# Token rows of a recurrence: identity products with the gate's columns beside them, or transpositions and products of eight columns

## The chip, the cores and the metric

The kernel runs on one core of a Trainium2 chip. The metric is device time in microseconds (us), the median of the runs of one kernel; lower is better.

## What is computed

A recurrence makes 2048 token states of width 256, a gate picks two of eight experts for each, and the experts' outputs are added to x. Cut to what matters:

```python
def step(prev_h, xw_t):                      # xw_t = (x @ Wx + b) at step t
    next_h = jnp.tanh(xw_t + prev_h @ Wh)
    return (next_h, next_h)
_, hs = jax.lax.scan(step, h0, jnp.swapaxes(xW, 0, 1))
...
logits = x_flat @ gate_w.T                   # x_flat: the states hs, [2048, 256]; gate_w: [8, 256]
top_v, top_i = jax.lax.top_k(logits, 2)
probs = softmax(top_v)
...
hidden = silu(x_flat @ wge.T) * (x_flat @ wue.T)
out   += we[:, None] * (hidden @ wde.T)      # we: this expert's weight for each token
...
return x + out
```

## The kernel before, in words

**The recurrence.** The long sequence is cut in 64 chunks for each of the two batches, so one step advances 128 states at once. The states lie transposed: two tiles of 128 features by 128 states (`hall[k][:, r, :]`, k = 0, 1). A step (loop at L668) is four products of 128 columns with `Wh` in two accumulators (L675), and two tanh on ACT (L694), which write the next states. Steps 8 to 27 use float16, the rest float32. From step 48 on the states of each step are kept: step 48 + r yields token tile r, r = 0 to 15.

**From states to rows.** One step after a tile's states exist, `route_tile` (L379) makes token rows of them. Its two products (L385) take the states as the stationary operand and `ig[:, k, :]` as the moving one, 136 columns: an identity of 128 columns, which turns the states, and the gate's eight columns beside it. The order in `ig` is identity and gate for k = 0, gate and identity for k = 1, so that both products write the same eight columns of one PSUM tile, 128 to 135, and the logits are summed there; columns 0 to 127 and 136 to 263 hold the two halves of the token's row. ACT then copies all 264 columns to SBUF (L387), to `gr["rows"]`. For tile 14, `before_copy` puts two transpositions of rows that were gathered earlier (`early_turn`, L516, L219), their cast on ACT and a subtraction on DVE ahead of that copy.

**What follows.** The tiles are routed in four groups (5, 3, 5 and 3 tiles). For each group DVE finds the two best logits (`route_max`, `route_choice`), ACT and DVE make the weights, PE counts the tokens of each expert with small float16 products (`route_position`, L433) and finds their places with others (`route_slots`, L479); SP's queue writes the rows to a table in DRAM (`rows_out`, L417), and POOL gathers from it by index (L493). The gathered rows are transposed again for the experts (`transpose_tokens`, L219), where each product is split in three terms (L759 for gate and up, L995 for down), and POOL adds the results to the output (L500).

**Order.** Each engine runs its instructions in the program's order. That order is written out by hand: `at(step, f)` files a function under a step number, and `run(step)` issues what is due, in the order of the numbers. `route_tile` for tile r stands at r + 49, so it is issued after the products, tanh and seeds of step r + 49; tile 15 is issued after the loop, ahead of the experts' first products. PSUM tiles for `route_tile` are `ptr`, two in turn. The lines touched by the change, and those next to it on PE, are L675 (recurrence), L385 (rows and logits), L433 and L479 (places), L219 (transpositions), L759 (the experts' first products). ACT, DVE and POOL instructions mostly appear as L57, that of a helper.

Of the kernel before, what the change touches and what calls it, by code (L numbers as in the profile page):

```python
# [19 lines left out]
P = 128  # L20
# [4 lines left out]
E = 8  # L25
# [35 lines left out]
def rnn_moe(ctx, tc, xP, cP, xT, xrows, h0T, Wx, Wh, b, gw, W, out):  # L61
    nc = tc.nc
    pe = tc.keep_in_program_order
# [12 lines left out]
    ig = cst.tile([P, 2, P + E], F32, name="ig")  # L76
    ident = cst.tile([P, P], F32, name="ident")
# [76 lines left out]
    def ptr_tile():  # L154
        return pl.ptp.tile([P, 512], F32, name="ptr", tag="ptr")
# [15 lines left out]
    def flat(t):  # L171
        return t.rearrange("p a c -> p (a c)")
# [29 lines left out]
    hall = [flat(t).bitcast(F32).rearrange("p (r c) -> p r c", r=R) for t in early["gu_g"]]  # L202
# [176 lines left out]
    def route_tile(gr, r, before_copy=lambda: None):  # L379
        i = r - gr["r0"]  # L380
        if i == 0:
            gr["mx"] = rt.tile([P, gr["n"], 8], F32, name="mx")
        pt = ptr_tile()[:, 0:ROW]
        for k in range(2):
            pe(nc.tensor.matmul(pt[:, k * P : (k + 1) * P + E], lhsT=hall[k][:, r, :], rhs=ig[:, k, :], start=(k == 0), stop=(k == 1), skip_group_check=True))  # L385
        before_copy()
        act.copy(gr["rows"][:, i, :], pt)  # L387

# [218 lines left out]
    for g, gr in enumerate(groups):  # L607
        for r in range(gr["r0"], gr["r0"] + gr["n"]):
            at(r + 49, route_tile, gr, r, *((lambda: early_turn(1),) if r == 14 else ()))
            at(maxima[r], route_max, gr, r)  # L610
# [57 lines left out]
    for s in range(S0, 64):  # L668
# [31 lines left out]
        if s in range(40, 48, 2):  # L700

            pt = ptr_tile()[:, 0:64]
# [585 lines left out]
```

## Time and profile before

| | us |
|---|---|
| median of 3 runs | 378.67 (378.03 to 378.75) |
| the profiled execution | 374.34 |
| its span in the profile | 372.5 |
| PE busy | 360.6 (97%) |
| PE weight loads busy | 344.6 (92%) |
| DVE busy | 221.4 (59%) |
| ACT busy | 198.6 (53%) |
| POOL busy | 121.4 (33%) |
| PE's share of the chain that ended last | 95% |

The profiled execution is one execution, 4.3 us shorter than the median of the runs; sums made from its rows stand against its own time. PE means TensorE's passes, PEld its weight loads, which overlap the passes. A pass's record lasts much longer than the distance to the next pass, since passes are pipelined. DVE is the vector engine, ACT the scalar engine, POOL the general one, SP the engine that issues plain DMAs. L385 is line 385 of the kernel. The chain that ended last is followed back from the end: at each step to what released it.

### The profile page before, as it was taken

Reading aid. Unit: us, or ns where it says so; the run is one execution under the profiler, and the core shown is the slowest. Engines: PE = TensorE matmul, PEld = TensorE weight load, DVE = VectorE, ACT = ScalarE, POOL = GpSimd, SP = SyncE. Lnnn points to the kernel's source line nnn. Section 1 sums busy time; section 2 is a strip of 40 time slices with the busy share of each in tenths; the row PEclk is TensorE's granted clock in tenths of the full one; section 3 lists DMA queues with packets and bytes.
Section 4 is the critical chain, followed back from the end, with each engine's and each line's share of the span. In section 5 each row is a group of like instructions: output and inputs, shape, how many; then the busy total and the mean of one; then the engine's idle time right before and its main releaser. Section 6 shows DMA issues by size and latency. Waiting matters only on the chain.

```text
span 372.5 us, 7262 instructions
## 1 busy us (share of the span) xinstructions
PE 360.6 (97%) x2743; PEld 344.6 (92%) x2743; DVE 221.4 (59%) x541; ACT 198.6 (53%) x458; POOL 121.4 (33%) x133
## 2 busy tenths in 40 slices
PE   7999999999999999999999999999999999999990
PEld 6999999999898889999999999999999999999890
DVE  6858737786577666745547554666646645663420
ACT  5776667634557446645456545556464465463320
POOL 3694001211872322862252503331033051005042
PEclk9999999999999999999999999999999999999997
DMA  8943234231482716745155333445215243004022
GB/s 263 472 173 123 111 108 117 69 80 31 80 282 61 246 45 191 147 173 141 31 141 143 60 113 101 81 143 143 94 25 138 95 147 39 2 0 53 0 24 35
DMA packets 17805, 42.11 MB, mean 113 GB/s; under 512 B 3995, under 2 KB 12243, under 8 KB 14643
## 3 DMA queue, kind: packets, MB, share of 16 engines
q1 hardware_dynamic: 11314, 32.59, 25.3%
q0 software_dynamic: 6448, 8.99, 14.2%
q8 instruction: 23, 0.38, 0.4%
q14 instruction: 20, 0.16, 0.1%
HBM read 35.15 MB, written 9.04 MB: 119 GB/s over the span
## 4 chain that ended last, share of the span: by engine, by line
PE 95%; DMA 1%; ACT 1%; POOL 1%; SPq 0%; issue 0%; POOLq 0%; ACTq 0%
PE pgu_t L759 49%; PE yb L995 21%; PE pgu_t L675 11%; PE ptr L328 3%; PE ptr L385 2%; PE ptr L219 2%; PE yb L946 2%; PE pgu_t L995 2%; DMA gu_u<-in_xP_dram 1%; PE ptr L995 1%; POOL out_dram L500 1%; PE pgu_t L310 1%; PE yb L479 0%; ACT gu_g L57 0%; PE yb L433 0%
## 5 line engine op out<-in xcount | busy, mean ns | idle before, releaser
L995 PE MATMUL yb<-wd,hh 128*128 128x256 f32 (+3 forms) x496 | 84.5, 283 | 0.5 <-ACT hh L57 0.5
L57 DVE TENSOR_TENSOR g<-g,pgu_t 128x256 f32<-128x256 f32 (+7 forms) x96 | 49.2, 512 | 59.1 <-PE pgu_t L759 51.4
L500 POOL DMA_INDIRECT out_dram<-y,si x27 | 44.4, 1646 | 108.3 <-ACT y L57 103.7
L57 ACT CAST hh<-g 128x256 fp32r<-128x256 f32 (+7 forms) x92 | 43.9, 477 | 64.4 <-DVE g L57 59.5
L759 PE MATMUL pgu_t<-xhi,gu_g 128*128 128x256 f32 (+7 forms) x384 | 76.9, 322 | 0.0
L759 PE MATMUL pgu_t<-xhi,gu_u 128*128 128x256 f32 (+7 forms) x384 | 76.7, 321 | 0.0
L57 ACT ACTIVATE g<-pgu_t 128x256 f32<-128x256 f32 (+7 forms) x96 | 44.0, 459 | 60.0 <-PE pgu_t L759 59.2
L995 PEld LDWEIGHTS yb<-wd,hh 128*128 128x128 f32 (+3 forms) x496 | 72.5, 185 | 2.1 <-ACT hh L57 0.7
L759 PEld LDWEIGHTS pgu_t<-xhi,gu_u 128*128 128x128 f32 x384 | 61.0, 188 | 3.7
L759 PEld LDWEIGHTS pgu_t<-xhi,gu_g 128*128 128x128 f32 x384 | 58.5, 189 | 2.3 <-ACT xhi L57 0.2
L57 DVE TENSOR_TENSOR hl<-g,hh 128x464 fp32r<-128x464 f32 (+5 forms) x52 | 30.5, 587 | 31.5 <-ACT hh L57 30.1
L493 POOL DMA_INDIRECT xg<-rows_d,gi x27 | 30.8, 1142 | 56.1 <-DVE cm L872 23.2
L759 PE MATMUL pgu_t<-xlo,gu_g 128*128 128x256 f32 (+7 forms) x192 | 46.2, 321 | 0.0
L759 PE MATMUL pgu_t<-xlo,gu_u 128*128 128x256 f32 (+7 forms) x192 | 46.1, 321 | 0.0
L995 PE MATMUL yb<-wd,hl 128*128 128x256 f32 (+3 forms) x152 | 42.7, 281 | 0.0
L759 PEld LDWEIGHTS pgu_t<-xlo,gu_g 128*128 128x128 f32 x192 | 32.4, 188 | 1.9
L759 PEld LDWEIGHTS pgu_t<-xlo,gu_u 128*128 128x128 f32 x192 | 32.3, 188 | 2.0
L675 PE MATMUL pgu_t<-h,wh 128*128 128x128 f32 (+1 forms) x224 | 28.8, 264 | 0.6 <-DVE wh L57 0.6
L995 PEld LDWEIGHTS yb<-wd,hl 128*128 128x128 f32 (+3 forms) x152 | 27.8, 183 | 0.0
L57 DVE TENSOR_TENSOR hh<-g,hh 128x256 fp32r<-128x256 f32 (+1 forms) x40 | 16.9, 424 | 17.8 <-ACT hh L57 16.8
L57 DVE TENSOR_TENSOR gu_u<-raw,gu_u 128x1024 fp32r<-128x1024 f32 (+1 forms) x18 | 20.3, 1127 | 0.9 <-ACT gu_u L57 0.9
L57 DVE TENSOR_TENSOR wd<-raw,wd 128x1024 fp32r<-128x1024 f32 (+1 forms) x18 | 19.9, 1105 | 0.9 <-ACT wd L57 0.9
(179 smaller groups left out, 478.8 us busy)
## 6 DMA issues: line engine op xcount, KB each, us to landing
raw<-in_W_dram SPq DMA_DIRECT2D x24, 1024.0 KB, 4.9
gu_u<-in_xP_dram SPq DMA_DIRECT2D x8, 256.0 KB, 4.8
rows_d<-gu_u SPq DMA_DIRECT2D x4, 320.0 KB
rows_d<-gu_u SPq DMA_DIRECT2D x4, 192.0 KB, 3.0
out_dram<-in_xrows_dram SPq DMA_DIRECT2D x1, 512.0 KB, 16.9
xg<-rows_d,gi POOLq DMA_INDIRECT x27
out_dram<-y,si POOLq DMA_INDIRECT x27
small<-in_cP_dram SPq DMA_DIRECT2D x1, 267.0 KB
```

Of the source, the lines that this page charges most:

```text
L57: return lambda *a, **k: self.tc.keep_in_program_order(f(*a, **k))
L219: pe(nc.tensor.transpose(pt[:, m, j, :], tiles[i][:, k * (P + E) : k * (P + E) + P], ident))
L310: pe(nc.tensor.matmul(bq(acc[s % 2][j])[:, :, sh:64], lhsT=wx16[:, k, j * P : (j + 1) * P], rhs=bq(x16[n][:, k, s % 2 * P : (s % 2 + 1) * ...
L328: pe(nc.tensor.matmul(pt, lhsT=wxs[a][:, k, j * P : (j + 1) * P], rhs=xparts[q % 2][c][:, k, :], start=(i == 0), stop=(i == len(terms) - 1)))
L385: pe(nc.tensor.matmul(pt[:, k * P : (k + 1) * P + E], lhsT=hall[k][:, r, :], rhs=ig[:, k, :], start=(k == 0), stop=(k == 1), skip_group_ch ...
L493: nc.gpsimd.indirect_dma_start(out=xg, out_offset=None, in_=rows[:, :], in_offset=bass.IndirectOffsetOnAxis(ap=idx, axis=0),)
L500: return nc.gpsimd.indirect_dma_start(out=out[:, :], out_offset=bass.IndirectOffsetOnAxis(ap=idx, axis=0), in_=y, in_offset=None, compute_ ...
L675: pe(nc.tensor.matmul(acc[s % 2][j], lhsT=w[:, k, j * P : (j + 1) * P], rhs=prev[k], start=False, stop=True, skip_group_check=True))
L759: pe(nc.tensor.matmul(pt, lhsT=a[i], rhs=b[j], start=(first and i + j + n == 0), stop=(j == 1 and n == len(lhs_rhs) - 1), skip_group_check ...
L946: pe(nc.tensor.matmul(yt, lhsT=wd[b][:, s, d * P : (d + 1) * P], rhs=u.hid[s][a], start=(s == 0 and n == 0), stop=(s == NIC - 1 and n == 2 ...
L995: pe(nc.tensor.matmul(yt[0:w, :], lhsT=h[a][:, i * P : i * P + w], rhs=wd[b][:, ic, :], start=(ic == 0 and first and n == 0), stop=(ic == ...
```

## The change

The two products of 136 columns become two products of eight columns (the gate's logits) and two transpositions of 128 columns (the row's halves), in the same PSUM tile and the same columns of it. The stationary operand of all four is the same pair of state tiles; the moving operand is a slice of `ig` that holds only the gate's columns, or `ident`, an identity tile that exists already. The copy on ACT and all that follows are as before; in the changed kernel, lines after this function are two higher (L385 becomes L385 for the products and L387 for the transpositions; L675 becomes L677, L759 becomes L761).

```diff
         pt = ptr_tile()[:, 0:ROW]
         for k in range(2):
-            pe(nc.tensor.matmul(pt[:, k * P : (k + 1) * P + E], lhsT=hall[k][:, r, :], rhs=ig[:, k, :], start=(k == 0), stop=(k == 1), skip_group_check=True))
+            pe(nc.tensor.matmul(pt[:, P : P + E], lhsT=hall[k][:, r, :], rhs=ig[:, k, (1 - k) * P : (1 - k) * P + E], start=(k == 0), stop=(k == 1), skip_group_check=True))
+        for k in range(2):
+            pe(nc.tensor.transpose(pt[:, k * (P + E) : k * (P + E) + P], hall[k][:, r, :], ident))
         before_copy()
         act.copy(gr["rows"][:, i, :], pt)
```

## The prediction

> **What bounds the kernel now.** I read the page first (PE busy 97% of the span, the chain that ended last 95% PE), then the stretch in which the changed function runs. It is called once per token tile, sixteen times, and its passes L385 start between 50.9 and 72.7 us. Busy time by stage:
>
> ```profile
> core 0: us, PE busy (x) PEld busy (x) DVE busy (x) ACT busy (x) POOL busy (x), PEclk, DMA share, GB/s
> 48.00:72.00 24.00, 23.86 (x243) 23.48 (x242) 15.01 (x83) 17.37 (x65) 3.89 (x8) 1.00 0.28 86
> ```
>
> PE is busy 23.86 of 24.00 us at a granted clock of 1.00; ACT has 6.6 us to spare and DVE 9. One would expect a recurrence to wait for its tanh. The chain of waits in order of time says that it does not:
>
> ```profile
> 54.27 0.89 PE pgu_t L675 x8
> 55.16 0.47 PE ptr L385 x4
> 55.62 0.89 PE pgu_t L675 x8
> 56.52 0.47 PE ptr L385 x4
> ...
> 70.38 0.36 PE yb L433 x15
> 70.74 0.55 PE pgu_t L675 x4
> 71.29 0.22 PE pgu_t L219 x2
> 71.51 0.45 PE pgu_t L675 x4
> ```
>
> A step is eight passes of the recurrence and four of L385, back to back, 0.89 + 0.47 = 1.36 us; neither tanh nor copy stands on the chain. So each ns that a tile adds to PE's stream or takes from it is a ns of the kernel, and what I need is how far apart passes start, not how long one takes (about 280 ns, nearly all overlapped with the next).
>
> **What a pass costs.** A float32 product is two records in the trace (32 products at L385, 64 records); a transposition is one (70 transpositions of token tiles, 66 + 4 records). Groups by form, mean ns last ahead of the idle time:
>
> ```profile
> L385 PE MATMUL ptr<-ig,gu_g 128*128 128x136 f32 x64 | 10.1, 281 | 0.0
> L385 PEld LDWEIGHTS ptr<-ig,gu_g 128*128 128x128 f32 x64 | 8.6, 191 | 0.0
> L219 PEld LDWEIGHTS ptr<-ident,xg 128*128 128x128 f32 x66 | 7.6, 140 | 0.4
> L433 PEld LDWEIGHTS <-ones 128*128 128x128 f16 x46 | 1.7, 96 | 0.0
> L995 PEld LDWEIGHTS yb<-wd,hl 128*112 128x112 f32 x8 | 1.4, 174 | 0.0
> L995 PEld LDWEIGHTS yb<-wd,hl 128*96 128x96 f32 x8 | 1.3, 161 | 0.0
> L995 PEld LDWEIGHTS ptr<-wd,hid 128*80 128x80 f32 x12 | 1.4, 148 | 0.0
> ```
>
> The weight loads are the point. Loads of 80, 96 and 112 columns take 148, 161 and 174 ns: 0.81 ns a column, so 128 columns occupy the load path some 104 to 110 ns, and about 80 ns of every record is latency. With that, a load of a transposition (140) occupies about 60 ns, a float16 load (96) about 16. The timeline confirms the 110 where nothing else can hide it, at the change from float16 passes to float32:
>
> ```profile
> 70.40 0.34 PE L433 MATMUL yb<-sel,ones 128*128 128x48 f16 x8
> 70.58 0.52 PEld L675 LDWEIGHTS pgu_t<-gu_g,wh 128*128 128x128 f32 x4
> 70.60 0.69 PE L675 MATMUL pgu_t<-gu_g,wh 128*128 128x128 f32 x4
> ```
>
> Four loads in 0.52 us, one of them 0.19, are (0.52 - 0.19) / 3 = 0.110 us apart, though the second had only to wait for the first. And in the chain the four passes after the float16 ones take 0.55 us where four others take 0.44 to 0.45: one bare load, 0.10 to 0.11 us. Narrow float16 passes themselves come every (0.34 - 0.17) / 7 = 0.025 us. Transpositions, from a burst of eight:
>
> ```profile
> 103.61 0.88 PEld L219 LDWEIGHTS ptr<-ident,xg 128*128 128x128 f32 x8
> 103.69 1.03 PE L219 MATMUL ptr<-ident,xg 128*128 128x128 f32 x8
> ```
>
> (1.03 - 0.27) / 7 = 0.108 us apart.
>
> **The change part by part.** Removed per tile: four passes of 136 columns, 0.47 / 4 = 0.1165 us each (191 ns loads hidden under the pass before), 0.466 us. Added: four passes of 8 columns (two products, two records each) and two transpositions of 128 columns. Six passes in place of four, and six loads.
>
> *The narrow passes.* No row shows a float32 product of 8 columns, so I bound it. From below: 0.025 us, the float16 row of L433. From above: 0.134, if a load began only when that 0.025 was over. I take 0.110, the bare load: it is a float32 load of 128 columns, the same that L385 makes now, and a pass of 8 columns is far too short to cover it. The first of the four is covered by the recurrence pass ahead of it, as today.
>
> *The transpositions.* From the last narrow pass to the first transposition I take 0.060 (its load; from above 0.110, if it cost as much as the others), from the first to the second 0.108, from the second to the recurrence's next pass 0.109 (its float32 load lies under the transposition).
>
> Sum per tile from its first pass to the recurrence's next: 3 x 0.110 + 0.060 + 0.108 + 0.109 = 0.607 us against 0.466: **+0.141 us**.
>
> Two rules of the Trainium skill would have it otherwise. Perfetto Trace Analysis, section Transposes, says that a logical transposition should use the transpose and not a product. The trace agrees as far as that goes: two passes of 0.108 for four of 0.1165, 0.25 us less a tile, 4.0 us in all if the logits were free. They were, as eight more columns of a pass that had its weights anyway; now they load the same states twice more, 3 x 0.110 + 0.060 = 0.39 us. And TensorE: Matmul & The Clock Gate, section Back-to-back issue gap, lists passes of 1 to 64 columns at about 60 cycles, 25 ns; with that the sum is 4 x 0.025 + 0.216 = 0.316, 0.150 less a tile. L433 has exactly those 25 ns, but with loads of 16 ns; with loads of 110 the figure doesn't hold, so I go by the load rows.
>
> *Which tiles are on the path.* Tiles 0 to 13 precede the recurrence or passes that it queues behind: fully paid. Tile 14 precedes two transpositions of gathered rows, and they start the next wait: paid. Tile 15 does not pay: after it PE waits for ACT's cast of those rows,
>
> ```profile
> 73.10 0.53 PEld L759 LDWEIGHTS pgu_t<-xhi,gu_g 128*128 128x128 f32 x4 [0.20 <-ACT xhi L57]
> ```
>
> and tile 15's passes sit in that wait. Its last pass begins at 72.83, the next could at 72.94, the load of L759 starts at 73.10 and is bare for 0.11: 0.27 us of room for 0.141. Were the cast not there, the sixteenth tile would cost its 0.141 too. Sum: 15 x 0.141 = **+2.1 us**.
>
> *What moves with it.* ACT's copy of the tile now waits for the second transposition; queued behind it on ACT is the next step's tanh, and PE waits for that. The last pass of the tile began 0.116 us ahead of the recurrence's next and took 0.279; now 0.109 ahead, taking 0.272: the copy lands at the same place in its step, and the step is 0.14 us longer, so tanh has room. The copy, the maxima and the DMAs keep forms and order on ACT, DVE, POOL and SP; no instruction passes another there. What they feed (gathered rows for L219, weights) gets later by what PE gets later. After 73 us the page has PE without a wait of note (0.5 us in one place), so the shift is carried to the end and neither grows nor is absorbed.
>
> The sum stands against the profiled execution: 374.34 us (span 372.5) becomes 376.4. The median of the runs is 4.3 us above that execution; I carry the difference over, 378.67 + 2.1 = 380.8 us, +0.6%.
>
> **The rivals.**
> - *Narrow float32 passes at the narrow rate* (the change ends faster): 0.316 for 0.466, 15 x -0.150 = -2.2, 376.4 us. For it: the 25 ns of L433. Against: the bare loads. It decides below (0.466 - 0.216) / 4 = 0.062 us per narrow pass; there the sign turns.
> - *Hidden:* if tanh set the step, 0.14 more on PE would fill its wait: 378.7. Against: no idle of PE in any step, and chain rows without tanh.
> - *Dearer loads:* narrow passes 0.134 apart and a transposition's load that isn't shorter: 3 x 0.134 + 0.134 + 0.108 + 0.109 = 0.753, +0.287 a tile, +4.3: 383.0. Against: L219's 140 ns, and the 0.110 between bare loads, in which no such drain shows.
>
> **How the numbers follow.** Mine 0.80, narrow rate 0.06, hidden 0.07, dearer 0.07. My own case runs from a narrow pass at 0.090 (+0.081 a tile, +1.2) to a transposition's load of 0.110 (+0.19, +2.9): 379.9 to 381.6. The three runs spread over 0.7 us, so I take 0.3 more below and 0.6 above, towards the dearer case: 379.6 to 382.2, leaving out the two cheaper cases and most of the dearer. A difference under about 0.2% (0.76 us) can't be told from none here. Slower 0.87 (mine and dearer), same 0.07, faster 0.06.
>
> **What would show it.** In the changed profile the loads of the narrow passes at 190 ns and those of the transpositions near 140; the chain of a step 0.89 + about 0.61; tile passes 64 narrow and 32 transpositions; the first pass of the gates at 75.2 in place of 73.1, and everything after it shifted alike. I am wrong if four narrow passes take much under 0.25 us with PE still the chain, or if a step stays at 1.36 us with idle time or tanh on the chain; and the size is wrong by 0.05 us a tile if the transposition's load is not short.

## The result, and the profile after

| | before | changed |
|---|---|---|
| median of 20 runs each | 375.47 us (373.48 to 378.75) | 378.00 us (376.19 to 380.81) |
| ratio, 95% interval | | 1.0066 (1.0043 to 1.009) |
| profiled execution, its span | 374.34, 372.5 | 377.32, 375.5 |
| from a tile's first pass to the gates' first pass | 22.17 us | 24.48 us |

The change costs 0.66%, about 2.5 us. The forecast was slower by 2.1 us, or 0.6%; but it named 380.8 us, and its range (379.6 to 382.2) does not hold 378.0. The difference was near, the level it was added to was not: the three runs of before that were shown had a median of 378.67, the seventeen that came with the result lie between 373.48 and 376.64.

The stretch of the last row, its ends in the kernel before and in the changed one:

```profile
50.93 0.40 PE L385 MATMUL ptr<-ig,gu_g 128*128 128x136 f32 x2
73.10 0.39 PE L759 MATMUL pgu_t<-xhi,gu_g 128*128 128x256 f32 x1
```

```profile
51.94 0.40 PE L385 MATMUL ptr<-ig,gu_g 128*128 128x8 f32 x3
76.42 0.39 PE L761 MATMUL pgu_t<-xhi,gu_g 128*128 128x256 f32 x1
```

Groups by form of the changed kernel, the narrow products (L385), the transpositions of states (L387) and, for comparison, those of gathered rows (L219); mean ns last ahead of the idle time:

```profile
L385 PEld LDWEIGHTS ptr<-ig,gu_g 128*128 128x128 f32 x64 | 8.4, 192 | 0.0
L387 PEld LDWEIGHTS ptr<-ident,gu_g 128*128 128x128 f32 x32 | 4.6, 183 | 0.0
L219 PEld LDWEIGHTS ptr<-ident,xg 128*128 128x128 f32 x66 | 7.6, 140 | 0.4
L385 PE MATMUL ptr<-ig,gu_g 128*128 128x8 f32 x64 | 8.2, 237 | 0.0
L387 PE MATMUL ptr<-ident,gu_g 128*128 128x128 f32 x32 | 6.6, 289 | 0.0
```

Sixty-four narrow passes and thirty-two transpositions, as counted. The narrow passes load for 192 ns, as the wide ones did with 191: eight columns in place of 136 save nothing there. The mean of 183 at L387 hides two sorts of load; one tile of the changed kernel, PE's loads, then its passes:

```profile
56.36 0.53 PEld L385 LDWEIGHTS ptr<-ig,gu_g 128*128 128x128 f32 x4
56.73 0.29 PEld L387 LDWEIGHTS ptr<-ident,gu_g 128*128 128x128 f32 x2
56.98 0.30 PEld L677 LDWEIGHTS pgu_t<-gu_g,wh 128*128 128x128 f32 x2
```

```profile
56.47 0.51 PE L385 MATMUL ptr<-ig,gu_g 128*128 128x8 f32 x4
56.84 0.42 PE L387 MATMUL ptr<-ident,gu_g 128*128 128x128 f32 x2
57.09 0.28 PE L677 MATMUL pgu_t<-gu_g,wh 128*128 128x128 f32 x1
```

Four narrow loads in 0.53 us, one of them 0.19, are 0.113 us apart. A pass that streams 8 columns cannot hide that, so the passes follow each other at the pace of their loads. The recurrence's next pass starts at 57.09, 0.62 us after the tile's first (0.466 before). The chain that ended last says the same, step after step:

```profile
55.12 0.35 PE ptr L385 x4
55.47 0.27 PE ptr L387 x2
55.74 0.89 PE pgu_t L677 x8
56.63 0.35 PE ptr L385 x4
56.98 0.27 PE ptr L387 x2
57.25 0.89 PE pgu_t L677 x8
```

0.89 us for the recurrence is untouched; 0.35 + 0.27 = 0.62 stands where 0.47 stood. From tile to tile it is 1.511 us, before 1.357. At the end of the stretch:

```profile
75.74 0.22 PE pgu_t L219 x2
75.96 0.35 PE ptr L385 x4
76.30 0.27 PE ptr L387 x2
76.57 0.94 PE pgu_t L761 x7
```

The gates now follow tile 15 with no gap worth the name: its passes fill the wait for ACT's cast. From the first pass of tile 15 to that of the gates it is 0.625 us in both kernels. The busy time of the stage confirms that PE is as full as before (23.86 of 24.00 us):

```profile
48.00:72.00 24.00, 23.86 (x244) 23.44 (x244) 13.22 (x68) 16.84 (x60) 2.39 (x6) 1.00 0.27 86
```

The two spans differ by 3.0 us, more than the 2.31 of the stretch. 1.0 us of it lies ahead of the first tile (51.94 against 50.93 us), where both kernels run the same instructions; after the gates' first pass the changed kernel is 0.3 us quicker here, and 0.4 us slower in its second profile. In the seven profiles of kernels that agree up to the first tile, its first pass starts between 50.89 and 52.37 us, so the stretch from there to the gates says more about the change than a pair of spans does.

### The profile page after: what moved, and what is told of

It reads as the page before. It is cut to its first block, busy times and chain, and to the rows that moved or that the text cites. A ratio compares the mean times of both kernels' runs of the same rounds, so it can differ in the third digit from the quotient of the medians.

```text
span 375.5 us, 7326 instructions
## 1 busy us (share of the span) xinstructions
PE 363.7 (97%) x2775; PEld 348.1 (93%) x2775; DVE 221.2 (59%) x541; ACT 199.4 (53%) x458; POOL 122.5 (33%) x133
## 4 chain that ended last, share of the span: by engine, by line
PE 95%; DMA 1%; POOL 1%; ACT 0%; SPq 0%; issue 0%; POOLq 0%
PE pgu_t L761 49%; PE yb L997 21%; PE pgu_t L677 11%; PE ptr L328 3%; PE ptr L219 2%; PE yb L948 2%; PE pgu_t L997 2%; PE ptr L385 1%; DMA gu_u<-in_xP_dram 1%; PE ptr L387 1%; PE ptr L997 1%; PE pgu_t L310 1%; POOL out_dram L502 1%; PE yb L481 0%; PE yb L435 0%
## 5 line engine op out<-in xcount | busy, mean ns | idle before, releaser
L761 PE MATMUL pgu_t<-xhi,gu_g 128*128 128x256 f32 (+7 forms) x384 | 76.9, 322 | 0.0
L761 PE MATMUL pgu_t<-xhi,gu_u 128*128 128x256 f32 (+7 forms) x384 | 76.5, 321 | 0.0
L761 PEld LDWEIGHTS pgu_t<-xhi,gu_u 128*128 128x128 f32 x384 | 61.0, 188 | 3.7
L761 PEld LDWEIGHTS pgu_t<-xhi,gu_g 128*128 128x128 f32 x384 | 58.6, 189 | 2.2
L495 POOL DMA_INDIRECT xg<-rows_d,gi x27 | 32.0, 1184 | 56.3 <-DVE cm L874 23.3
L761 PE MATMUL pgu_t<-xlo,gu_u 128*128 128x256 f32 (+7 forms) x192 | 46.3, 322 | 0.0
L761 PE MATMUL pgu_t<-xlo,gu_g 128*128 128x256 f32 (+7 forms) x192 | 46.0, 321 | 0.0
L761 PEld LDWEIGHTS pgu_t<-xlo,gu_u 128*128 128x128 f32 x192 | 32.4, 188 | 1.9
L761 PEld LDWEIGHTS pgu_t<-xlo,gu_g 128*128 128x128 f32 x192 | 32.4, 188 | 1.8
L677 PE MATMUL pgu_t<-h,wh 128*128 128x128 f32 (+1 forms) x224 | 29.3, 269 | 1.0 <-DVE wh L57 1.0
```

The source lines that it names most:

```text
L495: nc.gpsimd.indirect_dma_start(out=xg, out_offset=None, in_=rows[:, :], in_offset=bass.IndirectOffsetOnAxis(ap=idx, axis=0),)
L677: pe(nc.tensor.matmul(acc[s % 2][j], lhsT=w[:, k, j * P : (j + 1) * P], rhs=prev[k], start=False, stop=True, skip_group_check=True))
L761: pe(nc.tensor.matmul(pt, lhsT=a[i], rhs=b[j], start=(first and i + j + n == 0), stop=(j == 1 and n == len(lhs_rhs) - 1), skip_group_check ...
```

## The experiments

**Theory:** a narrow float32 pass costs its whole weight load, some 0.11 us, because nothing covers the next one; transpositions are cheap. **Rivals:** narrow passes are cheap and transpositions dear; or each pass has a price whatever stands beside it; or narrow passes are dear whatever their type. I read each run from the stretch between the first pass of tile 0 and the gates' first pass: 22.17 us before, 24.48 us changed. The first three kernels ran once each (383.64, 380.12 and 382.18 us, beside one run of before at 375.49), so for them only the trace counts; in all of them the granted clock of this stage was 1.00.

**The logits made twice.**

```diff
+        for _ in range(2):
+            for k in range(2):
+                pe(nc.tensor.matmul(pt[:, P : P + E], lhsT=hall[k][:, r, :], ...))
```

> The changed kernel with the two narrow products of each tile made twice (the second pair starts the sum anew). Read from the stretch between a tile's first pass and the first pass of the gates: 22.2 us before, 24.5 us changed. Theory (each narrow float32 pass costs a bare weight load, 0.111 us): 4 x 0.111 = 0.44 us more a tile, and some 0.33 for the last, which has 0.11 us of room: +7.0, the stretch 31.5 us. Rival (a narrow pass costs the 0.025 us of a float16 one, and the transpositions are what is dear): 16 x 0.10 = +1.6, 26.1 us.

Measured: the stretch is 31.54 us. In its chain a step is

```profile
54.36 0.79 PE ptr L386 x8
55.16 0.27 PE ptr L388 x2
55.43 0.89 PE pgu_t L678 x8
```

0.79 for eight narrow passes where 0.35 stood for four: 0.11 each. The rival of cheap narrow passes (26.1) falls.

**The transpositions made twice.**

```diff
+        for _ in range(2):
+            for k in range(2):
+                pe(nc.tensor.transpose(pt[:, k * (P + E) : k * (P + E) + P], hall[k][:, r, :], ident))
```

> The changed kernel with the two transpositions of each tile made twice. Theory (a transposition that follows another costs 0.108 us): 2 x 0.108 = 0.216 more a tile, 0.10 for the last: +3.3, the stretch of the tiles 27.8 us in place of 24.5. Rival (transpositions dear: what is left of 0.62 us after four narrow passes of 0.025, 0.26 each): 16 x 0.52 = +8.3, 32.8 us.

Measured: 27.89 us, and in the chain

```profile
55.46 0.89 PE pgu_t L678 x8
56.35 0.35 PE ptr L385 x4
56.70 0.49 PE ptr L388 x4
```

0.49 for 0.27: two more for 0.22 us. Transpositions are not what is dear.

**One part alone: narrow logits, rows by products.**

```diff
-            pe(nc.tensor.transpose(pt[:, k * (P + E) : k * (P + E) + P], hall[k][:, r, :], ident))
+            pe(nc.tensor.matmul(pt[:, k * (P + E) : k * (P + E) + P], lhsT=hall[k][:, r, :], rhs=ident, start=False, stop=True, skip_group_check=True))
```

> Only one part of the change: the logits by their own narrow products, but the rows by products with the identity (four passes of 128 columns) in place of transpositions. Theory: 4 narrow passes of 0.111, then 4 wide ones of 0.112: 0.89 us a tile against 0.616, 15 x 0.274 and some 0.16 for the last: +4.3, the stretch 28.8 us. So transpositions alone save 0.27 us a tile against products and the separate logits alone cost 0.42 against before. Rival (narrow passes at 0.025): 4 x 0.025 + 4 x 0.112 = 0.55 a tile, less than the changed kernel has, the stretch 23.4 us.

Measured: 28.81 us; from tile to tile 1.787 us, 0.276 more than with transpositions. So the change has two halves of opposite sign: transpositions for identity products save 0.28 us a tile, logits of their own cost 0.276 + 0.154 = 0.43. The saving is that of transpositions which stand behind narrow products.

**The changed kernel again**, beside the next three on one chip:

> The changed kernel once more, on the chip and in the rounds of the next three. Theory: +0.15 us on 15 tiles, +2.3 us against before, ratio 1.006. If the absolute level moves from set to set and the difference stays, then the level was what the forecast missed, not the cost.

Measured: 376.92 us against 375.03, ratio 1.0059 (1.0036 to 1.0082); the stretch 24.48 us once more. The ratio is not that of the two medians, which lie 1.9 us apart (2.5 in the first set); the intervals of both sets overlap. The level moved by a microsecond against the first set (378.00), the stretch did not.

**Each product followed by its transposition.**

```diff
         for k in range(2):
             pe(nc.tensor.matmul(pt[:, P : P + E], lhsT=hall[k][:, r, :], ...))
-        for k in range(2):
-            pe(nc.tensor.transpose(pt[:, k * (P + E) : k * (P + E) + P], hall[k][:, r, :], ident))
+            pe(nc.tensor.matmul(pt[:, k * (P + E) : k * (P + E) + P], lhsT=hall[k][:, r, :], rhs=ident, is_transpose=True, start=False, stop=True, skip_group_check=True))
```

> The changed kernel with each narrow product followed at once by the transposition of the same states, so that two of the four later weight loads lie under a transposition (narrow, narrow, transposition, twice). Theory (a load is bare only after a pass that is too short to cover it): 0.111 + 0.065 + 0.111 + 0.111 + 0.065 + 0.109 = 0.572 us a tile against 0.616, -0.7 us in the stretch of the tiles: 23.8 us, ratio to before about 1.0045. Rival (a price for each pass, whatever stands beside it): the same 24.5 us.

Measured: the stretch 23.81 us, from tile to tile 1.466 us (0.573 a tile). The ratio to before is 1.0048 (1.003 to 1.0066); it cannot be told from the changed kernel's 1.0059 by times, but the stretch can. The same passes in another order cost 0.045 us less a tile, so a price for each pass isn't it: what counts is whether a load lies under a pass long enough, and which load it is.

**Float16 logits.** Copies of the states, high halves alone, so that the logits are those of float16 operands:

```diff
+    def state_halves(r):
+        vec.tensor_copy(halves16(r, 0)[0], hall[0][:, r, :])
+        pool.tensor_copy(halves16(r, 1)[0], hall[1][:, r, :])
...
-            pe(nc.tensor.matmul(pt[:, P : P + E], lhsT=hall[k][:, r, :], rhs=ig[:, k, (1 - k) * P : (1 - k) * P + E], ...))
+            pe(nc.tensor.matmul(pt[:, P : P + E], lhsT=halves16(r, k)[0], rhs=gw16[:, k, 0, :], ...))
...
+            at(r + 48, state_halves, r)
```

> The logits from float16 copies of the states (one copied by DVE, one by POOL) and of the gate's weights: one pass a product in place of two, with the short float16 load. It leaves out the low halves, so that the logits are those of float16 operands. Theory (the load is the cost): 0.025 + 0.065 + 0.108 + 0.109 = 0.307 us a tile, 0.159 less than before: the stretch 19.8 us if ACT, which is busy 1.06 to 1.18 us of each step of then 1.20, keeps up; up to 21 if it doesn't; ratio to before 0.994 to 0.997. Rival (narrow passes are dear whatever their type, 0.111 each): 0.111 + 0.065 + 0.217 = 0.393, 21.1 us with nothing waiting on ACT.

Measured: 379.31 us, ratio 1.0108 (1.0069 to 1.0147), the stretch 25.64 us. As a faster kernel it is a miss, as a test of the load it isn't. Its chain before the first group of tiles is routed:

```profile
53.41 0.03 PE ptr L397 x2
53.44 0.28 PE ptr L399 x2
53.72 0.99 PE pgu_t L690 x8
54.71 0.03 PE ptr L397 x2
54.74 0.28 PE ptr L399 x2
55.02 0.89 PE pgu_t L690 x8
55.91 0.03 PE ptr L397 x2
```

From the first narrow product to the transpositions it takes 0.03 us: a step of 1.200 us, the 0.31 a tile that the short load predicts (the expected 0.307). Narrow passes aren't dear as such. Every second step carries 0.10 us more (0.99 for 0.89). The trace shows what its first load came after, the step's first tanh on ACT:

```profile
53.22 0.28 ACT L57 ACTIVATE gu_g<-pgu_t 128x128 f32<-128x128 f32 x1
53.55 0.63 PEld L690 LDWEIGHTS pgu_t<-gu_g,wh 128*128 128x128 f32 x5
```

The tanh ends at 53.50 and the load starts 0.05 us later, as in the other two such steps ahead of the first group; the load of the gates follows the end of ACT's cast at the same distance in both kernels of the comparison. In the kernel before, the same two rows are (in brackets ACT's idle time before it, and what the profile takes to have ended that)

```profile
52.26 0.28 ACT L57 ACTIVATE gu_g<-pgu_t 128x128 f32<-128x128 f32 x1 [0.23 <-DVE mx L57]
52.63 0.19 PEld L675 LDWEIGHTS pgu_t<-gu_g,wh 128*128 128x128 f32 x1
```

some 0.10 us apart, which leaves 0.05 us of room in every second step. So a tile that is shorter on PE by more than that brings tanh onto the path, and half of these steps take 1.30 us, not 1.20. This is read from times; no run tests it apart.

From the eighth tile on the copies take the gain back. What PE waited for in the stretch, from the waits (us in total, times, longest):

```profile
PE ptr L397 <- POOL x L57: 2.2, 1, 2.2
PE ptr L397 <- DVE x L57: 1.7, 2, 1.2
PE ptr L397 <- DVE last L57: 1.1, 1, 1.1
```

Five us of waits: POOL's copy stood behind gathers that waited for DVE's indices, DVE's copies behind the routing of earlier tiles.

**Float16 in halves, nothing but low x low left out.**

```diff
+    def state_halves(r):
+        for k in range(2):
+            vec.tensor_copy(halves16(r, k)[0], hall[k][:, r, :])
+        for k in range(2):
+            hi, lo = halves16(r, k)
+            pool.tensor_tensor(lo, hall[k][:, r, :], hi, ALU.subtract)
...
+        terms = [(k, a, b) for k in range(2) for a, b in ((0, 0), (0, 1), (1, 0))]
+        for m, (k, a, b) in enumerate(terms):
+            pe(nc.tensor.matmul(pt[:, P : P + E], lhsT=halves16(r, k)[a], rhs=gw16[:, k, b, :], start=(m == 0), stop=(m == 5), skip_group_check=True))
```

> The logits from float16 high and low halves of states and gate's weights, three products for each half of the features (high x high, high x low, low x high): six narrow float16 passes. The high halves by DVE, the low ones by POOL. Nothing is left out but low x low. Theory: 5 x 0.025 + 0.065 + 0.108 + 0.109 = 0.407 us a tile, 0.059 less than before: the stretch 21.3 us, ratio 0.9975, if DVE (0.4 us more a step) and POOL (0.8 us more a step) don't get in the way; if they do, PE waits at the narrow passes or at the gathered rows, and it is no faster than before.

Measured: 385.87 us, ratio 1.0307 (1.0274 to 1.034), the stretch 31.51 us. It got in the way, and more than I had priced. One round of the chain:

```profile
54.60 0.29 DVE pgu_t L57
54.90 0.27 DVE x L57 x2
55.17 0.82 POOL x L57 x2
56.21 0.29 PE ptr L404 x2
56.58 0.39 ACT gu_u L57
57.20 0.29 ACT gu_g L57
```

Rows under 0.27 us are left out. In every second step, at first, the recurrence has become a ring: DVE's copies, POOL's two subtractions, PE's narrow products and transpositions, its recurrence products behind them, and ACT's tanh, for which the next copies wait. The chain puts ACT's copy of the tile ahead of the tanh, but that copy ended at 56.97, over 0.2 us before; the records of the recurrence passes that the two tanh need end 0.04 us ahead of each. PE, full before, is busy 13.55 of the 15 us from 51 to 66.

The same trace rules out one more rival, that narrow passes are spaced by their sum in the same eight columns. Six of them, summed there too:

```profile
57.22 0.29 PE L402 MATMUL ptr<-gw,x 128*128 128x8 f16 x6
```

One lasts 0.17 us, so they are (0.29 - 0.17) / 5 = 0.024 us apart.

**The copies on POOL, ahead of the gathers, for some tiles.**

```diff
+        for k in range(2):
+            pool.tensor_copy(halves16(r, k)[0], hall[k][:, r, :])
...
+        if r < LIGHT:
+            ...
+        else:
+            for k in range(2):
+                pe(nc.tensor.matmul(pt[:, k * P : (k + 1) * P + E], lhsT=hall[k][:, r, :], rhs=ig[:, k, :], ...))
```

> Float16 logits (high halves alone, so the logits are those of float16 operands) with transpositions for tiles 0 to 12, both copies on POOL, issued ahead of the first gathers; tiles 13 to 15 by the products of before. In the run with copies on DVE and POOL the first steps took 1.20 and 1.30 us in turn and later ones waited for copies queued behind group work. Theory: with the copies out of DVE's queue, steps of 1.25 on average against 1.357, 13 x -0.107 = -1.4: the stretch of the tiles 20.8 us, ratio 0.996. Rival: POOL's queue (it waits for DVE's weights and index work) holds the copies up as DVE's did, and the stretch is 22.2 us or more.

> The same for tiles 0 to 8 alone, which leaves POOL free when it first waits for DVE's indices. Theory: 9 x -0.107 = -1.0: the stretch of the tiles 21.2 us, ratio 0.9975. Rival: held up copies, 22.2 us or more.

Measured: with 13 tiles the stretch is 22.63 us, ratio 1.0015 (0.9996 to 1.0033); with 9 tiles 21.85 us, ratio 0.9998 (0.998 to 1.0015). Neither can be told from before. With 13 tiles the rival's number holds (22.2 us or more), and PE waits 0.6 us for gathered rows. The second does gain 0.58 us over the first five steps and loses part of it when the first group is routed:

```profile
60.22 0.34 POOL ohp L58
60.62 0.28 POOL gu_u L58
60.91 0.76 POOL x L58 x2
61.72 0.18 PE ptr L398
```

POOL's copies stand behind its share of the group's weights (`ohp`), which waits for DVE. With 9 tiles theory and rival each had a part in it, and no version here beats the kernel before.

## Why the prediction was right and wrong

**Bound.** Right for longer steps: PE's stream sets the step, and a nanosecond added to it is one of the kernel. The step grew from 1.357 to 1.511 us and no wait took its place. The same nanosecond taken from it is not always one gained: tanh stands 0.05 us behind in every second step, as the run with float16 logits shows. The gates' first pass is at 76.42 us and not at 75.2, because the first tile starts 1.0 us later.

**The narrow passes.** Right, with the size a little low. I took 0.110 us for a bare float32 load; it is 0.111 to 0.113. The row that made the forecast was not one of a narrow float32 pass, for there was none, but the difference between loads of 80 and 112 columns and the first load after float16 passes.

**The transpositions.** The 0.060 us that I took for the first one's load is 0.065 in the trace: its record ends 0.162 us after that of the last narrow pass, and 0.097 of that is the difference between records that wait for no load (272 and 175 ns). The 0.108 for the second is 0.109 by the records' ends. The sum of 0.607 is 0.618 us measured, +0.154 a tile from step to step for my +0.141; over 15 tiles 2.31 for 2.1 us.

**Tile 15.** Right: 15 x 0.154 = 2.31 is the whole lengthening of the stretch; the sixteenth tile is hidden in the wait for the cast. Two slips of reading change nothing: L385's last pass starts at 72.8 us (72.7 is its load), and the 0.1165 is 0.466 / 4, not 0.47 / 4.

**Two rules of the Trainium skill.** Transpositions in place of products (Perfetto Trace Analysis, section Transposes) do save: 0.28 us a tile by the run with one part alone. The 25 ns of passes up to 64 columns (TensorE: Matmul & The Clock Gate, section Back-to-back issue gap) hold with float16 loads, where narrow passes came 25 to 28 ns apart, and not with float32 ones, where four took 0.35 us up to the first transposition's start. I had set that figure against my own sum without need: the same section says that in a stream of loads and passes both set the spacing, which is what the runs show.

**What failed.** The step in the prediction's words: "The median of the runs is 4.3 us above that execution; I carry the difference over, 378.67 + 2.1". I took a gap between the profiled execution and three runs for a constant of measurement. It was the level of those three runs: 20 runs have a median of 375.47 us, 1.1 above the profiled execution, and 375.47 + 2.1 is 377.6, in place of 378.00. The later sets have before at 375.49, 375.03 and 374.09. The range allowed 0.3 us below and 0.6 above for a spread of 0.7 seen in three runs; the level moved by three. Why those three runs were slow is open; the change has no part in it.

## What to carry to other kernels

A few columns more in a pass whose weights are loaded anyway are almost free (0.1165 us for 136 columns, 0.112 for the 128 of an identity product); the same eight columns as passes of their own cost a weight load each, and in float32 that is 0.11 us twice. Before splitting a product, count loads and ask for each which pass is long enough to hide it; order matters (0.045 us a tile here), and lighter loads help only if the copies that they need have an idle engine with nothing in front of them, and only as far as the next limit, here tanh, leaves room. And add a forecast difference to the level of many runs: when one execution and three runs disagree by 1.1%, the disagreement belongs in the range.

## What the runs showed of the hardware that I had not expected

- The load of a transposition that queues behind a bare load has a record of 224 ns in place of 141; the record of a narrow pass is 256 ns when it waited for its load and 175 when it didn't (first of the four). Some 81 ns of each is the wait, so records tell of a bare load if they are not averaged.
- The part ahead of the first tile took 1.0 us more in one profile of the changed kernel than in the other (51.94 and 50.89 us), nearly half of what the change costs, while the stretch of the tiles repeats within 0.01 us (24.48 twice).
